# A two-layer graph kernel: every engine in source order, dense rows beside the y blocks, nonzero counts on ScalarE

## Chip, cores, metric

One core of a Trainium2 chip. The metric is the device time of one execution in microseconds (us). The engines are called PE (TensorE), ACT (ScalarE), DVE (VectorE), POOL (GpSimd) and SP (SyncE, which here only issues transfers).

## The reference

2708 nodes with 1024 features, a sparse 0/1 adjacency matrix whose row degrees vary strongly, fp32 throughout:

```python
# layer 0: attention over the neighbours
q = x @ W_q.T + b_q;  k = x @ W_k.T + b_k;  v = x @ W_v.T + b_v
z = (q @ k.T) / sqrt(1024) * adj
z = where(z == 0.0, -10000.0, z)
x = layernorm(x + relu(softmax(z, axis=1) @ v))
# layer 1: plain graph convolution
x = layernorm(x + adj @ (x @ weight) + bias)
```

## The kernel before

It never forms the 2708 x 2708 scores. It computes M = W_q^T W_k once and y = x M + ... for 22 blocks of 128 rows ("y blocks", stored to DRAM as `y_d`). From each adjacency row it lists up to 24 neighbours, and it sorts the rows by degree into 22 blocks with 23, 11, 8, 7, ... 1, 0 neighbour slots. In each layer it gathers neighbour rows by indirect transfer, weights and sums them on DVE, turns the sum by transposes on PE, multiplies by W_v (or layer 1's weight) on PE, normalizes, and scatters. The 32 rows of highest degree (`HUB`) are worked as dense matrix products instead.

The lists and the y blocks (cuts are marked):

```python
            def list_columns(b):
                r0, n = b * P, rows[b]
                a = ix.tile([P, N], F32, name="a")
                load_rows(a, adj, r0, n)
                nc.vector.tensor_scalar(junk[:n], a[:n], 0.0, None, op0=ALU.not_equal, op1=ALU.add,
                                        accum_out=cnt[:n, b:b + 1])
                nc.vector.scalar_tensor_tensor(a[:n], a[:n], 1.0, iota[:n], op0=ALU.is_equal, op1=ALU.mult)
                # [cut: maxima of six ranges, then the 24 largest]

            def y_block(b):
                # [cut: loads of xt and xn, junka sums on ACT]
                nc.vector.scalar_tensor_tensor(junkc[:n], xn[:n], 1.0, u_bc[:n], op0=ALU.mult, op1=ALU.mult,
                                               accum_out=yo[:n, D:D + 1])
                nc.gpsimd.tensor_tensor(yo[:n, D:D + 1], yo[:n, D:D + 1], beta[:n], ALU.add)
                for h in range(NH):
                    hs = slice(h * HALF, (h + 1) * HALF)
                    po = p_o.tile([P, HALF], F32, name="po")
                    for c in range(DC):
                        nc.tensor.matmul(po, xt[:, c, :], m_sb[:, c, hs], start=(c == 0), stop=(c == DC - 1))
                    nc.vector.tensor_add(yo[:n, hs], po[:n], y_bc[:n, hs])
                m = n // 16 * 16
                nc.scalar.dma_start(out=y_d[r0:r0 + m], in_=yo[:m])
                if m < n:
                    nc.scalar.dma_start(out=y_d[r0 + m:r0 + n], in_=yo[m:n])
```

The end of the sort, the loop that mixes lists, y blocks and sort, and the norm that closes every block of both layers:

```python
                for b in range(NB):
                    put = nc.gpsimd.indirect_dma_start(
                        out=tab_d[:, :], out_offset=bass.IndirectOffsetOnAxis(ap=pos_i[:, b:b + 1], axis=0),
                        in_=rec[:, b, :], in_offset=None)
                    tc.declare_no_dep(put.ins, group="tab", reason="disjoint rows: positions are unique")
                    tc.add_to_no_dep_group("tab", put.ins)
                nc.sync.dma_start(out=tabs, in_=tab_d.rearrange("(b p) e -> p b e", p=P))

                for g in range(G):
                    nc.sync.dma_start(out=hub_row[g * HUB:(g + 1) * HUB], in_=tab_d[0:HUB, ROW:ROW + 1])
                for g in range(G):
                    gs = slice(g * HUB, (g + 1) * HUB)
                    nc.vector.tensor_scalar(hub_i[gs], hub_row[gs], float(G), float(g), op0=ALU.mult, op1=ALU.add)
                # [cut]
            for b in range(NB):
                for k in (2 * b, 2 * b + 1):
                    if k < NB:
                        list_columns(k)
                y_block(b)
                if 2 * b + 2 == NB:
                    sort_rows()

        def norm(t, sm, n):

            nm = stat.tile([P, 1], F32, name="lnm")
            nc.vector.tensor_scalar_mul(nm[:n], sm[:n], -1.0 / D)
            vs = stat.tile([P, 1], F32, name="vs")
            nc.scalar.activation(junks[:n], t[:n], AF.Square, bias=nm[:n], accum_out=vs[:n])
            ve = stat.tile([P, 1], F32, name="ve")
            nc.vector.tensor_scalar(ve[:n], vs[:n], 1.0 / D, EPS, op0=ALU.mult, op1=ALU.add)
            rstd = stat.tile([P, 1], F32, name="rstd")
            nc.gpsimd.tensor_tensor(rstd[:n], ve[:n], negh[:n], ALU.pow)
            nmr = stat.tile([P, 1], F32, name="nmr")
            nc.gpsimd.tensor_tensor(nmr[:n], nm[:n], rstd[:n], ALU.mult)
            nc.scalar.activation(t[:n], t[:n], AF.Identity, bias=nmr[:n], scale=rstd[:n])
```

The dense rows' scores are part of layer 0's jobs, and layer 1's residual add is on POOL at the block's end:

```python
        jobs = [17, 0, "hub", 16, 0, 15, 0, "one", 14, 1, ...]     # [cut]

        def finish1(b, po, xr):                                     # layer 1
            # [cut]
                nc.gpsimd.tensor_tensor(xr[:n], xr[:n], bias1[:n], ALU.add)
                # [cut: two evictions on DVE, each adding xr and summing]
            norm(t, sm, n)
            scatter(out, b, n, t, "out")
```

The source above is not the order in which an engine works: without a further word, the builder's scheduler reorders the instructions of each engine. With `tc.manual_schedule()` each engine issues them as the source has them.

## Time and profile before

| what | before |
|---|---|
| time, median of 4 runs beside the changed kernel | 1364.74 us (1360.12 to 1367.37) |
| weights and M; y blocks | 155.7 us; to 495 us |
| layer 0; layer 1 | 450 us; 389 us |
| busy PE, DVE, POOL, ACT | 1195.5, 802.4, 503.5, 284.2 us |
| mean granted PE clock | 0.928 |

The lines of the page, the stage windows and PE's waits of this kernel are in the prediction below. Read them so: PE is busy 88% and is the engine to feed. A wait line names the engine, what it wanted to do, what it waited for, the total, how often, and the longest. The main reading below compares DVE's waits inside layer 0. Here are three of them in this kernel:

```profile
DVE t L521 <- PE po L419: 69.2, 12, 16.4
DVE junkv L439 <- DMA g<-in_x_dram,tabs: 30.2, 19, 8.3
...
DVE ve L431 <- ACT junks L429: 6.9, 6, 1.3
```

They are the wait for PE's product, for gathered rows, and for ACT's Square (the sum of squares in `norm`).

### The profile page before, as it was taken

The numbers are of one execution on the slowest core, as the hardware profiler recorded it, in microseconds if no ns is written. First come the engines' busy times: TensorE is split into PE (matmuls) and PEld (weight loads), VectorE is DVE, ScalarE is ACT, GpSimd is POOL, SyncE is SP. The second block draws the span as 40 slices with busy tenths as digits, with TensorE's granted clock in tenths as the row PEclk, the third lists the DMA queues.
The fourth block names the chain that finished last, engine by engine and source line by source line (L and its number), as shares of the span: only waits on it lengthen the run. The fifth ranks groups of instructions, "written<-read, shape, count | busy, mean of one in ns | idle before, by whom it ended". The sixth has DMA issues, their size and how long they took to land. (4 is left out here: it accounts for less than half of the span.)

```text
span 1361.2 us, 10176 instructions
## 1 busy us (share of the span) xinstructions
PE 1195.5 (88%) x3225; PEld 542.9 (40%) x3225; DVE 802.4 (59%) x1448; ACT 284.2 (21%) x697; POOL 503.5 (37%) x494
## 2 busy tenths in 40 slices
PE   6999978899989996987891999997788899988996
PEld 4544433344434442442250444443332344433442
DVE  5899989993131216795078898941452355656611
ACT  2300101122121212221021233232110113121321
POOL 1000000000600036362167677511773558778711
PEclk7899989899999997998986899999888899988998
DMA  7434376534254359868778787711889866677511
GB/s 288 144 134 152 141 298 233 173 121 139 63 158 119 82 208 416 343 220 241 202 282 278 256 278 249 253 46 47 277 289 298 272 221 210 232 227 237 184 47 49
DMA packets 92391, 275.79 MB, mean 203 GB/s; under 512 B 12372, under 2 KB 34228, under 8 KB 88596
## 3 DMA queue, kind: packets, MB, share of 16 engines
q0 software_dynamic: 44896, 160.96, 34.5%
q1 hardware_dynamic: 44368, 102.95, 23.8%
q10 hardware_dynamic: 3064, 11.14, 2.1%
q8 instruction: 27, 0.44, 0.1%
q14 instruction: 36, 0.29, 0.1%
HBM read 241.38 MB, written 33.63 MB: 202 GB/s over the span
## 5 line engine op out<-in xcount | busy, mean ns | idle before, releaser
L279 PE MATMUL po<-m_sb,xt 128*128 128x512 f32 x704 | 312.2, 606 | 23.0 <-DMA xt<-in_xT_dram 23.0
L419 PE MATMUL po<-wv_sb,rT 128*128 128x512 f32 x704 | 317.8, 607 | 1.7 <-DVE rT L657 1.7
L419 PE MATMUL po<-w_sb,rT 128*128 128x512 f32 x672 | 303.4, 607 | 17.1 <-DVE t L737 17.1
L279 PEld LDWEIGHTS po<-m_sb,xt 128*128 128x128 f32 x704 | 136.3, 195 | 196.2 <-issue 177.7
L419 PEld LDWEIGHTS po<-wv_sb,rT 128*128 128x128 f32 x704 | 134.0, 195 | 170.0 <-issue 164.7
L419 PEld LDWEIGHTS po<-w_sb,rT 128*128 128x128 f32 x672 | 127.8, 194 | 177.6 <-issue 162.4
L381 POOL DMA_INDIRECT g<-in_x_dram,tabs x122 | 151.0, 1238 | 96.7 <-issue 46.1
L721 DVE SCALAR_TENSOR_TENSOR r<-g,valid,r 128x1024 f32<-128x1024 f32 x79 | 126.5, 1602 | 66.9 <-DMA g<-x_d,tabs 65.2
L381 POOL DMA_INDIRECT g<-x_d,tabs x122 | 140.8, 1154 | 34.4 <-issue 29.9
L439 DVE SCALAR_TENSOR_TENSOR junkv<-yg,g 128x1024 uint8<-128x1024 f32 x100 | 122.3, 1223 | 31.0 <-DMA g<-in_x_dram,tabs 30.2
L433 POOL TENSOR_TENSOR rstd<-ve,negh 128x1 f32<-128x1 f32 (+1 forms) x44 | 39.6, 901 | 222.9 <-DVE ve L431 222.7
L429 ACT ACTIVATE junks<-t,lnm 128x1024 uint8<-128x1024 f32 (+1 forms) x44 | 50.6, 1150 | 327.8 <-DVE lnm L427 323.5
L220 PE MATMUL po<-wk_o,wq_o 128*128 128x512 f32 x256 | 112.3, 598 | 0.0
L264 ACT ACTIVATE junka<-xt 128x128 f32<-128x128 f32 x176 | 54.4, 309 | 258.2 <-DMA xt<-in_xT_dram 197.8
L487 DVE SCALAR_TENSOR_TENSOR r<-g,pr,r 128x1024 f32<-128x1024 f32 x79 | 100.5, 1282 | 6.9 <-ACT r L485 6.3
L271 POOL MEMSET yo<- 128x4 f32 x22 | 2.2, 102 | 267.4 <-DMA y_d<-yo 205.7
L410 PE MATMUL tr<-ident,r 128*128 128x128 f32 x336 | 51.2, 300 | 53.3 <-DVE e L460 28.6
L436 ACT ACTIVATE t<-t,nmr,rstd 128x1024 f32<-128x1024 f32 (+1 forms) x44 | 54.6, 1240 | 144.8 <-POOL nmr L435 140.4
L272 DVE SCALAR_TENSOR_TENSOR junkc<-xn,u_bc 128x1024 uint8<-128x1024 f32 (+1 forms) x22 | 26.9, 1224 | 92.6 <-POOL yo L271 72.0
L249 DVE MAX8 few<-a 128x8 f32<-128x75 f32 (+3 forms) x132 | 76.9, 614 | 0.1
L737 DVE SCALAR_TENSOR_TENSOR t<-po,g 128x512 f32<-128x512 f32 x42 | 28.4, 686 | 79.4 <-PE po L419 79.4
L521 DVE TENSOR_TENSOR t<-po,bias_bc 128x512 f32<-128x512 f32 (+1 forms) x44 | 30.2, 686 | 75.4 <-PE po L419 75.4
(189 smaller groups left out, 948.5 us busy)
## 6 DMA issues: line engine op xcount, KB each, us to landing
a<-in_adj_dram SPq DMA_DIRECT2D x21, 1354.0 KB
xm<-in_xT_dram SPq DMA_DIRECT2D x8, 1354.0 KB
y_d<-yo ACTq DMA_DIRECT2D x21, 514.0 KB
xt<-in_xT_dram SPq DMA_DIRECT2D x21, 512.0 KB
xn<-in_x_dram SPq DMA_DIRECT2D x21, 512.0 KB
g<-in_x_dram SPq DMA_DIRECT2D x24, 448.0 KB
g<-x_d SPq DMA_DIRECT2D x24, 448.0 KB
wq_i<-in_wqT_dram SPq DMA_DIRECT2D x8, 512.0 KB
```

The source lines that it names most:

```text
L220: nc.tensor.matmul(po, wq_o[:, o, i * P:(i + 1) * P], wk_o[:, o, hs], start=(o == 0), stop=(o == DC - 1))
L249: nc.vector.max(few[:n, i * 8:(i + 1) * 8], a[:n, cuts[i]:cuts[i + 1]])
L264: nc.scalar.activation(junka[:, :P], xt[:, c, :], AF.Copy, accum_out=xs[:, c, b:b + 1])
L279: nc.tensor.matmul(po, xt[:, c, :], m_sb[:, c, hs], start=(c == 0), stop=(c == DC - 1))
L381: nc.gpsimd.indirect_dma_start(out=g[:n], out_offset=None, in_=src, in_offset=bass.IndirectOffsetOnAxis(ap=tabs[:n, b, word:word + 1], axi ...
L410: nc.tensor.transpose(tr[:, k, :], r[:, c * P:(c + 1) * P], ident)
L419: nc.tensor.matmul(po, rT[:, c, :], w[:, c, h * HALF:(h + 1) * HALF], start=(c == 0), stop=(c == DC - 1))
L429: nc.scalar.activation(junks[:n], t[:n], AF.Square, bias=nm[:n], accum_out=vs[:n])
L436: nc.scalar.activation(t[:n], t[:n], AF.Identity, bias=nmr[:n], scale=rstd[:n])
L439: nc.vector.scalar_tensor_tensor(junkv[:n], yg[:n, :D], scale, xg[:n], op0=ALU.mult, op1=ALU.mult, accum_out=s)
L487: nc.vector.scalar_tensor_tensor(r[:n], xg[j][:n], pr[:n, j:j + 1], r[:n], op0=ALU.mult, op1=ALU.add)
L721: nc.vector.scalar_tensor_tensor(r[:n], xg[:n], valid[:n, b, j:j + 1], r[:n], op0=ALU.mult, op1=ALU.add)
```

## The change

The intent was to replace the scheduler's order by one planned by hand. PE is to find its next operand ready at every step, and the dense rows' work is to be taken out of layer 0, where they caused PE's longest waits.

```diff
-    with es:
+    with es, tc.manual_schedule():
```
```diff
+            nc.scalar.activation(junk[:n], a[:n], AF.Sign, accum_out=cnt[:n, b:b + 1])
+            nc.scalar.activation(junk[:n], a[:n], AF.Relu, scale=-1.0, accum_out=neg[:n, b:b + 1])
-                nc.vector.tensor_scalar(junk[:n], a[:n], 0.0, None, op0=ALU.not_equal, op1=ALU.add,
-                                        accum_out=cnt[:n, b:b + 1])
```

On ACT the count takes two passes: the Sign pass counts, and the Relu pass finds rows with negative entries, for which that count would not hold.

```diff
+EARLY = 13      # lists beside M; the other nine in y blocks 0 to 6
+SORT = 7        # sort around the eighth y block
+G1, G2 = 6, 8   # gather buffers (15 before); adjacency buffers 2 -> 3, xn 2 -> 1, r 4 -> 3, yg 3 -> 2
+        for b in range(SORT):
+            while done < EARLY + (NB - EARLY) * (b + 1) // SORT:
+                list_columns()
+                done += 1
+            y_block(b)
+        sort_begin()
+        y_block(SORT)
+        sort_end()
+        # [cut]
+        for b in range(SORT + 1, NB):
+            y_block(b)
+            # [cut: at chosen b, one piece of the dense rows: scores in 24 steps, softmax, two chunks of rows]
+        wv_sb = wv_pool.tile([P, DC, D], F32, name="wv_sb", tag="v")
+        nc.sync.dma_start(out=wv_sb, in_=wvT.rearrange("(c p) n -> p c n", p=P))
```

The body of both layers becomes one loop. `work.run()` issues the next job's gathers and then computes the job issued before. A job is one or several pieces of at most eight neighbours of a block.

```diff
+            for i, b in enumerate(order):
+                xr = residual(b)                       # gather, POOL
+                credit += STEP - end_cost
+                # [cut: work.run() until the next block is there, and while there is credit]
+                for h in range(NH):
+                    product(b, turned[b], h, po)       # 16 matmuls
+                    if h == 0 and i + 1 < len(order):
+                        turned[order[i + 1]] = turn(order[i + 1])   # transposes on PE, copies on ACT
+                for hook in hooks.get(i, ()):
+                    hook()                             # a chunk of the dense rows
+                if past is not None:
+                    end(*past)                         # finish0 or finish1 of the block before
+                past = b, po, xr
```

Between the scatters of the sort a one-element memset was added on POOL as a spacer.

## The prediction

> **What bounds the kernel now.** I read the busy shares and the 40 slices first, then TensorE's waits, then busy time by stage, then each engine's timeline around the waits.
>
> ```profile
> PE 1195.5 (88%) x3225; PEld 542.9 (40%) x3225; DVE 802.4 (59%) x1448; ACT 284.2 (21%) x697; POOL 503.5 (37%) x494
> PE   6999978899989996987891999997788899988996
> DVE  5899989993131216795078898941452355656611
> PEclk7899989899999997998986899999888899988998
> ```
>
> TensorE leads; the rest is its idle time (166 us) and the clock it loses after each gap. Where DVE shows 9 (slices 3 to 10 and 20 to 25), TensorE dips.
>
> The stages, as windows cut where TensorE's operand changes (columns: window, length, busy time per engine, granted clock, DMA share, GB/s):
>
> ```profile
> 0.00:155.70 155.70, 140.75 (x409) 73.22 (x410) 135.78 (x258) 28.58 (x70) 3.55 (x11) 0.91 0.48 175
> 155.70:320.00 164.30, 145.24 (x331) 63.93 (x330) 142.12 (x272) 30.92 (x148) 5.77 (x20) 0.94 0.57 194
> 320.00:495.00 175.00, 169.70 (x398) 75.08 (x396) 39.17 (x94) 36.58 (x178) 26.16 (x46) 0.99 0.38 110
> 495.00:945.00 450.00, 382.61 (x1137) 172.38 (x1138) 300.48 (x569) 109.42 (x189) 226.50 (x206) 0.92 0.72 245
> 961.00:1350.00 389.00, 356.24 (x951) 157.55 (x949) 181.09 (x247) 73.76 (x107) 233.33 (x202) 0.94 0.66 216
> ```
>
> They are: weights and M; y blocks 0 to 9; y blocks 10 to 21; layer 0; layer 1. At full clock the timeline of TensorE has 0.43 us per fp32 matmul instruction, so 13.7 us a y block (32 of them) and 14.6 a block of the layers (with transposes). Layer 0 needs 22 x 14.6 = 321 us plus some 45 for the dense ("hub") rows, and takes 450. Layer 1 needs 21 x 14.6 = 307 plus 31, and takes 389. So 80 and 50 us are there to be won. The y blocks lose 36, and I expect the turn between the layers (16) and the tail (11) to stay. TensorE's waits, whole run:
>
> ```profile
> PE tr L410 <- DVE e L460: 28.6, 1, 28.6
> PE po L279 <- DMA xt<-in_xT_dram: 23.0, 4, 8.2
> PE po L419 <- DVE t L737: 17.1, 5, 5.8
> PE tr L410 <- DVE r L719: 16.2, 2, 15.1
> PE tr L403 <- DVE part L610: 14.5, 2, 8.7
> PE mm L553 <- DMA yg<-y_d,tabs: 10.2, 1, 10.2
> PE po L607 <- DMA g<-in_x_dram: 7.8, 1, 7.8
> ```
>
> The dense rows in layer 0 bring the waits on yg, g and part, and behind them DVE falls late (28.6).
>
> **What the Trainium skill says.** (1) TensorE: Matmul & The Clock Gate, Part 1: after an idle window of about 3.4 us the array runs at half rate until about 3.4 us of work. The trace agrees: the eight transposes after the 15 us gap at 960 took 1.94 us, later ones 1.04. A long gap therefore costs about 2 us more than itself. (2) The same page, "Architectural detail": ACT and DVE are strict FIFO, and TensorE only pulls weight loads ahead. The trace of before agrees as far as it goes: ACT's junka waited 21.3 us on DVE's yo, because the y_d transfer stood ahead of it in ACT's order. This decides my prediction: source order makes every wait hold all that stands behind it. (3) DMA: Bandwidth & Descriptors, "Anatomy of one DMA": a semaphore wait happens on the issuing sequencer. SP's waits agree (151 us behind DVE's few). (4) ScalarE: Activation LUTs, "Step-by-step": 0.833 ns per element for any function. Here 128x128 took 309 ns and 128x1024 took 1150, a slope of 0.94; I use that.
>
> **Part by part.**
>
> *Weights and M.* All 32 groups of transposes now precede M. A pair took 2.65 us: 7.3 + 16 x 2.65 = 50; M is 256 x 0.43 = 110, plus 2 of cold clock: 162, against 155.7. The count leaves DVE (21 x 2.95 = 62 us), and ACT gets two passes of 2708: 1.15 + 1684 x 0.94 ns = 2.73, plus 0.19 for the sum, so 5.9 us a list. Thirteen lists fit beside M (8.4 us apart; DVE needs 2.97 + 3.3 for the maxima + 1.0). The last list's passes stand ahead of the y_bc copies on ACT, so y block 0 starts near 170.
>
> *y blocks 0 to 7, nine lists among them.* Here I see a closed ring. ACT reaches the passes of the next list only after the y_d issue of this block, which waits for DVE's eviction; DVE may overwrite `a` only after ACT's passes; SP, in order, loads the next adjacency block only when the maxima are done, and xn (now one buffer) behind it; DVE needs xn before it evicts. The landing time is in the timeline:
>
> ```profile
> 220.44 0.33 SPq L144 DMA_DIRECT2D a<-in_adj_dram  x1
> 220.87 0.38 SPq L260 DMA_DIRECT2D xt<-in_xT_dram  x1
> 227.91 0.31 ACT L264 ACTIVATE junka<-xt 128x128 f32<-128x128 f32 x1 [15.88 <-DMA xt<-in_xT_dram]
> ```
>
> Half a megabyte behind an adjacency block landed 7.5 us after the first issue; I take 7.2. Round the ring: 0.5 (issue) + 5.9 + 6.25 + 7.2 + 1.25 (junkc) + 1.35 (eviction) = 22.5 us, 7.3 more with two lists, 16.3 when no adjacency load is left (23.6 with two). Evictions end at 193, 215, 238, 268, 290, 306, 330. TensorE, two blocks ahead at most, wants 13.7 and starves.
>
> *Sort.* Before, the positions to the tables was:
>
> ```profile
> 342.76 1.15 POOL L339 DMA_INDIRECT tab_d<-rec,pos_i  x1 [0.17 <-issue]
> 369.65 0.97 POOL L339 DMA_INDIRECT tab_d<-rec,pos_i  x1 [0.30 <-issue]
> 371.80 0.38 SPq L344 DMA_DIRECT2D tabs<-tab_d  x1
> 375.96 0.14 DVE L350 TENSOR_SCALAR hub_i<-hub_row 32x1 int32<-32x1 int32 x1 [3.35 <-DMA hub_row<-tab_d]
> ```
>
> That is 33 us, and the scheduler had put evictions between. In source order hub_i follows at once on DVE, so no eviction passes, and xn of block 8 waits on SP behind the tables and five xm loads. Sort start and block 7 end at 339; 6.6 of DVE, 29 to 30 of POOL, 6 of landing, 9 until xn lands, 3 of junkc and eviction: block 8 is evicted near 394. TensorE has two blocks (27 us) to fill 55. Blocks 0 to 9, done at 320 before, are done at 394.
>
> *Blocks 10 to 21 with the dense rows.* 12 x 13.7 = 165, 2 cold, and TensorE's dense work: two dozen score steps 10, hub_y 128 small matmuls at 0.11 = 14, transposes and flips 5, two chunks of rows 8, waits for softmax and copies 8: 45. Ends at 606. Then wv (4 MB) is issued only after the last block and behind row chunks: 6.3 MB at some 380 GB/s (the slices peak at 416) is 17 us, about 18 idle: 624.
>
> *Layer 0.* The dense stalls are gone, but DVE still has 100 scores x 1.30 + 79 sums x 1.28 + 66 for the 22 ends + some 30 small = 327 us, against TensorE's 321 + 20 for the remaining chunks. In order, each end's variance waits for ACT's Square, about 1.5 us (22.4 us over 17 waits before), so DVE needs 327 + 33 + 15 for gathers = 375, little of it done in the wv gap. Layer 0: 376 instead of 450, ends near 1000. *Turn* 15. *Layer 1*: 338 plus 12 of waits, since POOL needs (J+1) x 1.43 + 6.9 us a block, over 14.6 for J above 4: 350 instead of 389. *Tail* 12.
>
> Sum: 606 + 18 + 376 + 15 + 350 + 12 = 1377. Gains 74 + 39; losses 6 + 74 + 38 + 18. I have counted each wait as fully exposed; xn's rows are contiguous and may land 2 to 3 us sooner, six times, and layer 0 may run nearer TensorE's 341. I take 22 off: **1355 us**.
>
> **Rivals.** (A) The plan holds: TensorE never waits over a few us; y and dense rows end near 520, layer 0 takes 345, layer 1 345: about 1250. For it: idle and cold clock are all that separates the stages from their work, and the parameters look tuned. Against: the ring and the hub_i wait follow from order alone. (B) In-order DVE is worse than I think in layer 0: each residual gather, exp and Square stops it; DVE's 300 us busy took 390 before with free order. Layer 0 then stays near 430: about 1420. (C) The wait for tables is mostly covered and the ring is as computed: 1310.
>
> **Range and chances.** A and C below, B above, my sum at 1377 as it stands: 1280 to 1415. Faster by over 2% means below 1339: 0.40; between 1339 and 1394: 0.38; slower: 0.22.
>
> **What would show it.** Right: evictions of y blocks 1 to 4 some 22 us apart; DVE waiting on ACT's passes (near 6 us) and on xn; one DVE wait of over 30 us on hub_row, a TensorE gap of 25 to 30 behind it; a gap of 15 to 20 on wv; no wait on yg or part; layer 0 under 400. Wrong: y blocks 13.7 us apart from the start (rival A), or layer 0 over 420 with DVE waiting on junks (rival B).

## The result, and the profile after

1557.37 us, median of 4 runs (1555.97 to 1558.47), against 1364.74. The ratio is 1.1415, with a 95% interval of 1.1378 to 1.1452: slower.

The page of the kernel after, its busy line, two of its 40-slice rows and the granted clock:

```profile
PE 1210.8 (78%) x3415; PEld 564.3 (36%) x3415; DVE 744.7 (48%) x1416; ACT 397.6 (26%) x785; POOL 497.4 (32%) x521
...
PE   7998976574999983967742487899485878899896
...
DVE  5899554822102211377557477776114425443321
...
PEclk9999997887989996978876789999797888999998
```

PE's work has hardly grown (15 us), but its share of the span fell from 88% to 78%: the change added idle time. The mean granted clock fell from 0.928 to 0.881.

The stage windows of the kernel after, cut where PE's operand changes (M; y blocks 0 to about 9; the rest with the dense rows; layer 0; layer 1; columns as in the prediction):

```profile
0.00:139.70 139.70, 131.86 (x402) 66.12 (x403) 111.44 (x214) 81.48 (x84) 3.48 (x10) 1.00 0.53 197
139.70:370.00 230.30, 155.02 (x342) 68.18 (x340) 118.60 (x281) 81.76 (x189) 27.89 (x64) 0.84 0.38 125
370.00:592.00 222.00, 212.42 (x767) 107.37 (x767) 41.01 (x79) 46.27 (x226) 3.88 (x26) 0.93 0.51 144
618.80:1099.40 480.60, 354.48 (x952) 164.95 (x952) 310.27 (x550) 104.49 (x170) 215.82 (x203) 0.86 0.56 194
1120.40:1545.00 424.60, 356.71 (x954) 157.65 (x954) 154.71 (x278) 75.16 (x107) 229.55 (x198) 0.91 0.57 194
```

PE's longest waits, whole run of the kernel after:

```profile
PE tr L465 <- DVE r L542: 93.0, 8, 38.7
PE po L324 <- DVE yo L325: 54.2, 5, 27.7
PE po L797 <- DVE t L891: 39.3, 10, 8.3
PE po L797 <- DVE t L578: 33.1, 3, 14.9
...
PE po L797 <- DMA wv_sb<-in_wvT_dram: 26.5, 1, 26.5
```

The waits on yg and part in layer 0 are gone, as planned. In their place PE waits for DVE: for the row sum it is to transpose (r, 93.0 us) and for PSUM, where its products gather, to be evicted, that is copied out by DVE (54.2, 39.3 and 33.1 us). Here is every wait of DVE inside layer 0 of the kernel after:

```profile
DVE junkv L494 <- DMA g<-in_x_dram,tabs: 69.4, 16, 32.3
DVE ve L486 <- ACT junks L484: 46.1, 21, 7.5
DVE r L542 <- ACT r L540: 22.8, 18, 1.6
DVE t L578 <- PE po L797: 17.6, 4, 6.2
DVE rden L532 <- ACT pr L527: 7.6, 16, 0.8
DVE den L529 <- ACT pr L527: 1.9, 3, 0.6
```

They add up to 165.4 us. With the 310.3 us that DVE is busy in this window that is 475.7 of its 480.6 us. (Work and waits fill the window of any engine, so this sum alone does not make DVE the bound.) What points to DVE is who waits for whom: in this window DVE waits for PE 17.6 us, and PE waits for DVE 126.1 (93.0 and 33.1). In the kernel before, DVE waited 69.2 us for PE's product in layer 0.

One of the waits for Square, seen in the timeline of layer 0 of the kernel after (start, duration, engine, line, instruction, and in brackets the idle time before it and what ended it):

```profile
856.11 0.15 DVE L482 TENSOR_SCALAR lnm<-sm 128x1 f32<-128x1 f32 x1
...
861.35 1.07 ACT L466 COPY rT<-tr 128x512 f32<-128x512 f32 x2 [10.60 <-PE tr L465]
...
862.31 1.16 ACT L484 ACTIVATE junks<-t,lnm 128x1024 uint8<-128x1024 f32 x1
...
863.59 0.15 DVE L486 TENSOR_SCALAR ve<-vs 128x1 f32<-128x1 f32 x1 [7.33 <-ACT junks L484]
...
863.83 1.50 POOL L488 TENSOR_TENSOR rstd<-ve,negh 128x1 f32<-128x1 f32 x1 [10.46 <-DVE ve L486]
```

DVE has the mean at 856.1. ACT could take the square of 1.15 us at once, but ahead of it in ACT's order stand the two copies of the next block's transposes, which wait for PE. The square starts at 862.3; DVE, whose next instruction needs its sum, stands 7.33 us, and POOL, which needs DVE's result, stands 10.46 us with the next gathers behind it. The later waits for gathers (69.4 us in all) may be partly made here; e4 below, which takes most of the waits for Square away, lowers them by only 9.7 us.

And DVE's longest wait in the whole kernel after, and one block end of layer 1 with an instance of it:

```profile
DVE t L891 <- POOL g L887: 175.5, 20, 31.1
...
1304.80 0.94 POOL L433 DMA_INDIRECT g<-x_d,tabs  x1 [0.30 <-issue]
1305.76 2.34 POOL L887 TENSOR_TENSOR g<-g,bias 128x1024 f32<-128x1024 f32 x1
1308.14 0.69 DVE L891 SCALAR_TENSOR_TENSOR t<-po,g 128x512 f32<-128x512 f32 x1 [11.91 <-POOL g L887]
```

POOL's add of residual and bias needs nothing that is late. But it is in the source after the next jobs' gathers, so POOL issues those first, about 1.25 us apart. PE's finished product waits in PSUM, and DVE waits 11.91 us for an add of 2.34 us. Over layer 1 this wait comes 20 times and takes 175.5 us of DVE's time.

### The profile page after: what moved, and what is told of

Read it like the earlier page. It is cut to its first block, busy times and chain, and to the rows that moved or that the text cites. A ratio compares the mean times of both kernels' runs of the same rounds, so it can differ in the third digit from the quotient of the medians. Undisturbed runs are those within 1.5% of the kernel's fastest.

```text
span 1556.6 us, 10644 instructions
## 1 busy us (share of the span) xinstructions
PE 1210.8 (78%) x3415; PEld 564.3 (36%) x3415; DVE 744.7 (48%) x1416; ACT 397.6 (26%) x785; POOL 497.4 (32%) x521
## 5 line engine op out<-in xcount | busy, mean ns | idle before, releaser
L797 PE MATMUL po<-wv_sb,rT 128*128 128x512 f32 x704 | 323.5, 618 | 59.6 <-DVE t L578 33.1
L324 PE MATMUL po<-m_sb,xt 128*128 128x512 f32 x704 | 322.6, 619 | 54.2 <-DVE yo L325 54.2
L797 PE MATMUL po<-w_sb,rT 128*128 128x512 f32 x672 | 312.2, 621 | 39.4 <-DVE t L891 39.3
L433 POOL DMA_INDIRECT g<-in_x_dram,tabs x125 | 130.2, 1042 | 106.8 <-PE mm L697 42.3
L494 DVE SCALAR_TENSOR_TENSOR junkv<-yg,g 128x1024 uint8<-128x1024 f32 x100 | 122.5, 1225 | 71.8 <-DMA g<-in_x_dram,tabs 69.4
L433 POOL DMA_INDIRECT g<-x_d,tabs x122 | 118.0, 967 | 75.3 <-issue 35.1
L488 POOL TENSOR_TENSOR rstd<-ve,negh 128x1 f32<-128x1 f32 (+1 forms) x44 | 49.2, 1118 | 240.5 <-DVE ve L486 240.4
L891 DVE SCALAR_TENSOR_TENSOR t<-po,g 128x512 f32<-128x512 f32 x42 | 27.4, 689 | 177.1 <-POOL g L887 175.5
L873 DVE SCALAR_TENSOR_TENSOR r<-g,valid,r 128x1024 f32<-128x1024 f32 x79 | 101.5, 1284 | 8.8 <-DMA g<-x_d,tabs 6.3
L466 ACT COPY rT<-tr 128x512 f32<-128x512 f32 (+1 forms) x84 | 45.5, 581 | 219.6 <-PE tr L465 219.4
L317 DVE SCALAR_TENSOR_TENSOR junkc<-xn,u_bc 128x1024 uint8<-128x1024 f32 (+1 forms) x22 | 26.9, 1223 | 140.9 <-DMA xn<-in_x_dram 137.3
L465 PEld LDWEIGHTS tr<-ident,r 128*128 128x128 f32 x336 | 43.7, 155 | 138.3 <-issue 136.1
L217 DVE SCALAR_TENSOR_TENSOR a<-a,iota 128x2708 f32<-128x2708 f32 (+1 forms) x22 | 65.3, 2968 | 42.3 <-ACT junk L216 42.3
```

Source lines behind the costliest of these rows:

```text
L433: nc.gpsimd.indirect_dma_start(out=dst[:n], out_offset=None, in_=src, in_offset=bass.IndirectOffsetOnAxis(ap=at, axis=0))
L465: nc.tensor.transpose(tr[:, k, :], r[:, c * P:(c + 1) * P], ident)
L494: nc.vector.scalar_tensor_tensor(junkv[:n], yg[:n, :D], scale, xg[:n], op0=ALU.mult, op1=ALU.mult, accum_out=s)
L797: nc.tensor.matmul(acc, rT[:, c, :], w[:, c, h * HALF:(h + 1) * HALF], start=(c == 0), stop=(c == DC - 1))
L873: nc.vector.scalar_tensor_tensor(r[:n], xg[j - cut[i]][:n], valid[:n, b, j:j + 1], r[:n], op0=ALU.mult, op1=ALU.add)
```

## The experiments

My theory after the result was ORDER: the loss is source order itself, in which each wait holds all that stands behind it on its engine, and most of it lies in the two layers (Square, and POOL's add). Its rivals were that the plan's contents cost the time whatever the order (the dense rows beside the y blocks, fewer buffers, counts on ACT), and that single stage gaps (tables, wv) or the ring in the first y blocks carry it.

**e1, the order alone.** The changed kernel with the scheduler's order:

```diff
-    with es, tc.manual_schedule():
+    with es:
```

> The changed kernel with its plan, buffers and operations as they are, but the instruction order of each engine left to the scheduler again (one word taken out). Theory ORDER (the loss comes from strict source order: waits that hold what stands behind them): DVE's waits on POOL's residual add (175 us), on the tables (33) and on Square (80) mostly go, both layers come under 450 and 390, and the time is 1290 to 1400. Rival PLACE (the loss comes from where the plan puts work and from its smaller gather buffers): stays above 1480, with the same waits under other names.

Measured 1349.94 us, ratio to before 0.9905 (0.9874 to 0.9935): 207 us less than with source order. Layer 0 took 422 us (528 to 950), layer 1 took 362 (973 to 1335). Two of DVE's waits in layer 0 of this run:

```profile
DVE junkv L494 <- DMA g<-in_x_dram,tabs: 37.7, 21, 5.0
...
DVE ve L486 <- ACT junks L484: 8.2, 7, 1.3
```

The wait for Square in layer 0 is 8.2 us instead of 46.1, by order alone; over the whole run it is 36.6 instead of 79.9, and DVE's wait for POOL's add is 26.1 instead of 175.5. This shows that source order costs the whole loss, and that the plan under a free order is about 1% from the kernel before.

**e2, source order on the kernel before**, with the same spacers as the change:

```diff
-    with es:
+    with es, tc.manual_schedule():
```

> The kernel before, all else unchanged, in strict source order (and one small memset before each table scatter, which the order needs to build). ORDER: it is slowed by 10% or more, since its source was written for a scheduler: 1500 to 1750. PLACE: within 4% of the kernel before, 1310 to 1420.

Measured 2073.14 us, ratio 1.5214 (1.5166 to 1.5262). The direction was expected, the size was above my range: PE waited 445.9 us for DVE's row sums alone, and layer 0 took some 860 us. So the plan is a good deal better than a source never meant to be issued as it stands (2073 to 1557). It just does not reach what the scheduler does with either source.

**e3, POOL's add earlier.** The add of residual and bias moved ahead of the next block's residual gather and jobs:

```diff
+                if ready is not None and past is not None:
+                    ready(*past)                # the POOL add of the block before
                 xr = residual(b)
```

> The changed kernel with POOL's add of residual and bias in layer 1 issued one step earlier, ahead of the next gathers in POOL's order; nothing else. If DVE's 175 us of waiting for that add is what makes layer 1 long (425 us), layer 1 falls to 360 to 390 and the time by 35 to 65 us, to 1490 to 1525. Rival: POOL is simply full in layer 1 (230 us busy and waits of its own round its ring), the wait moves to gathers, and the time falls by less than 15 us.

Measured 1506.19 us, ratio 1.1041: 51 us less than after. Layer 1, from the start of its first product to that of its last, took 370 instead of 422 us, and DVE's wait for this add fell from 175.5 to 30.1 us. A third of the wait taken away became time. DVE had slack in layer 1 (154.7 us busy of 424.6), and part of it came back as waits for gathers (the first row's from 38.0 to 70.7 us).

**e4, the norm in two parts.** The variance, its power, the scaling and the scatter are issued after the next step's jobs, so that DVE has other work while ACT squares. It needs a fourth `r` buffer (the kernel before had four too), so a fixed order has to be planned together with its buffers; the fourth buffer without the move was not run.

```diff
             nc.scalar.activation(junks[:n], t[:n], AF.Square, bias=nm[:n], accum_out=vs[:n])
+            return t, nm, vs, n
+        def norm_end(t, nm, vs, n):
             ve = stat.tile([P, 1], F32, name="ve")
 ...
+                flush()                         # norm_end and scatter of the block before
                 po = []
```

> The changed kernel with each block's normalisation cut in two: the part behind ACT's Square (variance, rstd, scaling, scatter) is issued one step later, after the next step's gathers and sums; one more r buffer, which that needs. If the chain DVE-ACT-DVE-POOL in the middle of the queues costs what the waits say (DVE 80 us on Square, POOL 225 on the variance, which holds the gathers), DVE's wait on Square falls under 15, its wait on gathers in layer 0 (69) at least halves, and the time falls by 50 to 110 us. Rival: those waits only fill slack that the busiest engine leaves: less than 20 us.

Measured 1471.97 us, ratio 1.0791: 85 us less, the largest single term. From first to last product layer 0 took 430 instead of 480 us, and layer 1 386 instead of 422. In the whole run:

```profile
DVE junkv L497 <- DMA g<-in_x_dram,tabs: 59.7, 14, 30.7
...
DVE ve L489 <- ACT junks L484: 25.7, 11, 6.8
```

The wait for Square fell from 79.9 to 25.7 us, not under 15 as expected (in layer 0 alone it is 6.1). The waits for gathers fell from 69.4 only to 59.7, so the part of my expectation that had them halve missed too.

**e5, wv earlier.** W_v and the bias loaded before y block 18 instead of after the last.

```diff
         for b in range(SORT + 1, NB):
+            if b == SORT + 11:
+                # bias_bc and wv_sb: tile and load, moved here from after the loop
             y_block(b)
```

> The changed kernel with the loads of wv and its bias issued four y blocks earlier on SP; nothing else. ORDER: the 26.5 us that TensorE waits for wv, and the cold clock behind it, go: 22 to 30 us less, 1527 to 1536. Rival: layer 0 is bound by DVE, which has the gap to catch up, so that a later wait gives it back: less than 10 us.

Measured 1555.38 us, ratio 1.1427 (1.1396 to 1.1458): 2 us less than after by the medians, but in e5 to e8 the kernel before was also 3.5 us faster (1361.26), and the kernel after was not run again. By the ratio (1.1415 for the kernel after) nothing is gained, which is what the rival expected (under 10 us). PE's wait of 26.5 us on wv is gone, and in its place in the waits of PE stands this one:

```profile
PE po L798 <- DVE rT L807: 17.1, 1, 17.1
```

DVE reaches rT only after the single-neighbour blocks, whose gathers come late: POOL stood 13.37 us until PE had used a chunk of the dense rows and its gather buffers came free. Two waits lay side by side; taking one away left the other. The last product of the y blocks also began 9 us later.

**e6, tables later.** The load of the sorted tables and hub_i moved behind y block 10, so that DVE could evict while POOL scatters.

```diff
+            if b == SORT + 3:
+                sort_tabs()                     # tabs, hub_row, hub_i, degs, valid
+                # the gathers of a0 and x0 and the first load_xm, moved here
```

> The changed kernel with the part of the sort behind the table scatters (reading the tables, hub_i, valid, the two dense gathers, the first xm loads) issued three y blocks later. ORDER: DVE's 33 us wait on hub_row and TensorE's 27.7 us gap behind it go, 24 to 34 us less, 1523 to 1534. Rival: the dense rows then start later and push into layer 0: under 10 us.

Measured 1552.29 us, ratio 1.1401 (1.1376 to 1.1425): 5 us less by the medians, 2 by the ratio, and so not clear of noise. PE's gap of 27.7 us went down to 8.7. But DVE did not evict while POOL scattered. In place of its 33.3 us for hub_row stands:

```profile
DVE junkc L317 <- POOL yo L316: 28.3, 1, 28.3
```

This is the next block's memset of `yo`, which stands in POOL's order behind the scatters. So the wait changed its name and lost only 5 us; what it would be worth if it were gone was not tested. New waits of PE of 6.0 and 5.2 us came for the rows gathered later, so layer 0 began at 611.5 instead of 618.8 us, and two more us were given back behind it.

**e7, the ring opened.** ACT stores a y block only after the next list's passes, and xn of the next block is loaded before the next adjacency block.

```diff
+            while stores:
+                stores.pop(0)()                 # y_d issue, after the next Sign and Relu
 ...
             load_x()
+            if b < SORT:
+                load_xn(b + 1)
```

> The changed kernel with the ring of the first y blocks opened at two places: each xn load is issued ahead of the next adjacency load on SP, and the y_d store of a block behind the next list's two passes on ACT; nothing else. ORDER: of the 42 us that TensorE waits in y blocks 3 to 7 (and at the sort) 30 or more go, 30 to 50 us less with the cold clock: 1507 to 1527; DVE's 137 us wait on xn falls by 70 or more. Rival: DVE's lists themselves are the bound there: under 15 us.

Measured 1501.8 us, ratio 1.1036: 55 us less by the medians, 52 by the ratio, a little more than expected. Layer 0 began at 563.2 instead of 618.8 us, so all that was won in the y blocks was kept. DVE's wait for ACT's passes fell from 42.3 to 8.5 us; its wait for xn fell from 137.3 only to 115.1, where I had expected 70 less. (A wait of 28.4 us on an eviction, that of the tables, is still there.) This shows the ring of the prediction and its price.

**e8, all five together**, still in source order: the edits of e3 to e7.

> The changed kernel, still in source order, with all five moves at once: residual add early, normalisation in two parts, wv early, tables late, ring open. ORDER: the single gains (51 and 85 measured, some 25, 28 and 40 expected) add up, less some 20 that two of them share: 1330 to 1370, level with the kernel before. Rival: each freed wait only uncovers the next: above 1420.

Measured 1389.76 us, ratio 1.0212 (1.0192 to 1.0233): 168 us less than after, where the single gains add up to 198. It stayed 20 us above the range that I had given. Layer 1 took 365 us (362 in free order). Layer 0 took 429 from its first to its last product (480 in the kernel after, 430 in e4, 422 in e1). Two of DVE's waits in this layer 0, and the window, which runs 7 us past the start of the last product:

```profile
DVE junkv L517 <- DMA g<-in_x_dram,tabs: 54.6, 11, 26.5
...
DVE ve L509 <- ACT junks L504: 7.5, 5, 1.6
```

```profile
556.00:992.00 436.00, 346.93 (x952) 160.24 (x952) 310.90 (x555) 103.38 (x173) 190.61 (x207) 0.90 0.62 218
```

The wait for Square is down to 7.5 us. DVE's 310.9 us and all its waits (111.0) make 421.9 of these 436 us, of which its waits for gathers are the half. One wait of PE is new here: it waits for ACT's copies of the transposes, 26.0 us in layer 0, where the kernel after has none:

```profile
625.45 1.24 ACT L514 ACTIVATE t<-t,nmr,rstd 20x1024 f32<-20x1024 f32 x1 [2.33 <-POOL nmr L513]
626.59 1.04 ACT L486 COPY rT<-tr 128x512 f32<-128x512 f32 x2
627.21 8.56 PE L837 MATMUL po<-wv_sb,rT 128*128 128x512 f32 x16 [18.28 <-ACT rT L486]
```

The second part of the norm, which e4 moved, now puts ACT's scaling of one block, which needs DVE's variance and POOL's power, ahead of the copies for the next. So the move took away one wait of this kind and made another; a better place for it was not tried.

**e9, all five in the scheduler's order** (e8 without `tc.manual_schedule()`).

> The changed plan with all five moves in the source, and the order left to the scheduler. If the moves help it as they help source order, 1300 to 1335, below both kernels. Rival: the scheduler already placed these instructions so, and layer 0 is held by DVE (297 us busy in 431): within 1% of the free order without them, 1337 to 1363.

Measured 1348.35 us, ratio 0.9917 (0.9881 to 0.9952), the same as e1. With its own order the scheduler gains nothing from the five edits, as the rival expected.

**e10, e11, e12, the counts alone.** e10 is e1 with the counts put back on DVE; e11 is the kernel before with only the counts moved to ACT; e12 is the changed kernel with the counts put back on DVE. The edit of e11:

```diff
-                nc.vector.tensor_scalar(junk[:n], a[:n], 0.0, None, op0=ALU.not_equal, op1=ALU.add,
-                                        accum_out=cnt[:n, b:b + 1])
+                nc.scalar.activation(junk[:n], a[:n], AF.Sign, accum_out=cnt[:n, b:b + 1])
+                nc.scalar.activation(junk[:n], a[:n], AF.Relu, scale=-1.0, accum_out=neg[:n, b:b + 1])
 ...
+                nc.vector.scalar_tensor_tensor(capn, neg, 0.0, capn, op0=ALU.is_gt, op1=ALU.max)
```

> Free order, with the nonzero counts put back on DVE (62 us more there, 119 us less on ACT). If the counts are worth something, DVE's lists end later, the sort with them, and the time rises by 10 to 30 us over the free order, 1360 to 1380. Rival: DVE has slack in the y blocks (128 us busy of 371), under 7 us.

> The kernel before with only the nonzero counts moved to ACT. There DVE was full from 68 to 300 us and SP's loads of xt waited behind its lists (TensorE waits 23 us on xt): 8 to 25 us less than before, 1338 to 1356. Rival: the y blocks lose only what xt's landing costs anyway, under 5 us.

> The changed kernel in source order with the counts back on DVE. In the ring of the first y blocks 5.9 us of ACT become 2.95 of DVE, some 27 us less over nine lists; beside M the list takes DVE 10.3 us against 8.4 between two, so DVE comes some 25 us late out of M: within 20 us of the changed kernel, 1537 to 1577. Rival (the passes on ACT are what makes the ring long): 30 us or more less.

Measured: e10 1370.44 us, ratio 1.0077 (1.0045 to 1.011); e11 1337.66 us, ratio 0.9838 (0.9803 to 0.9872); e12 1575.96 us, ratio 1.1587 (1.1546 to 1.1629). Moving the counts to ACT is worth about 20 us in every order, by the medians: 22 in the kernel before, 20 in free order (e10 against e1, of another call), 19 in source order (e12 against the kernel after, of another call); by the ratios, 22 to 23 in each. In e11 the gain of 1.6% is clear of noise. In e11 the y blocks end at 468 us instead of 493. PE's wait there for its operand was 23.0 us in the kernel before; with the counts on ACT it is:

```profile
PE po L281 <- DMA xt<-in_xT_dram: 4.3, 1, 4.3
```

The likely chain, not tested further: DVE finishes each list sooner, the two adjacency buffers come free sooner, and SP, which loads both in turn, reaches the next xt sooner. The counts are the only part of the change that was shown to gain. The rest of the plan together costs about 10 us in free order: e1, which has the counts on ACT too, takes 1350, and e9 1348, where e11 takes 1338.

**e13, e14, e15, what still holds layer 0.** Open after e8 was whether layer 0 is held by (a) the order of the heavy blocks, whose work comes before DVE has any lead, or (b) the number of gather buffers. e13 is e8 with the heavy blocks two places later. e14 is e11 with the same order. In both, the list of jobs is moved with it (not shown). e15 is e8 with `G2` 10 instead of 8.

```diff
-        order = last + single[::-1] + [17, 16, 15, 0, 14, 1, 13, 2, 12, 3, 11, 4, 10, 5, 9, 6, 8, 7]
+        order = last + single[::-1] + [17, 16, 15, 14, 13, 0, 12, 1, 11, 2, 10, 3, 9, 4, 8, 5, 7, 6]
```

> All five moves in source order, and in layer 0 the 23-slot block two places later, the other heavy blocks one light block later each. (a) early DVE work holds layer 0: the one wait of 36 us behind that block shrinks to under 15 and the time falls by 15 to 35 us, 1355 to 1375. (b) gather buffers: within 8 us of 1390.

> The kernel before with the counts on ACT and the same later place of the heavy blocks in layer 0. (a): the 28.6 us wait behind that block mostly goes: 12 to 30 us less than the counts alone, 1308 to 1326, below every version so far. (b): within 6 us of 1338.

> All five moves in source order with 16 gather buffers instead of 14. (b): DVE's wait on gathers in layer 0 falls by 20 us or more and the time by 10 to 25, 1365 to 1380. (a): within 6 us of 1390.

Measured: e13 1388.72 us, ratio 1.0189 (1.0165 to 1.0213); e15 1386.45 us, ratio 1.0181 (1.0153 to 1.0208); both the same as e8. In e13 PE's single wait of 36.0 us on DVE became several of at most 8.5 us, and one of 11.9 on ACT came up: PE's waits in layer 0 are 91.4 us in all against 100.2, and the time is the same. In e15 DVE waited 55.7 us for gathers against 54.6. So neither (a) nor (b) holds; what does was not tested. PE's waits for ACT's copies are in both runs (27.1 and 24.9 us). e14 took 1332.18 us, ratio 0.9785 (0.9762 to 0.9809). It has the lowest median of all, ahead of both kernels of the case, but is only about 5 us below e11, where I had expected more, and the two ran in different calls. Whether the later heavy blocks gain anything over e11 stays open.

## Why the prediction was wrong

Predicted 1355 us with 1280 to 1415; measured 1557. The sum before my discount was 1377. By its own terms:

| step | predicted | measured | difference |
|---|---|---|---|
| weights and M | 162 | 139.7 | -22 |
| y blocks 0 to about 9 | 232 (to 394) | 230.3 (to 370) | -2 |
| the other y blocks, dense rows | 212 | 222 | +10 |
| wait for wv | 18 | 26.5 | +8 |
| layer 0 | 376 | 480.6 | +105 |
| turn | 15 | 21 | +6 |
| layer 1 | 350 | 424.6 | +75 |
| tail | 12 | 11.6 | 0 |

The differences and the 22 us taken off make 202, all of the miss.

- *Right: the ring.* Evictions of the first y blocks began at 171.3, 192.9, 214.5, 243.6, 263.9, 279.5 and 302.6, so they are 21.6, 21.6, 29.1, 20.3, 15.6 and 23.1 us apart; I had 22, 23, 30, 22, 16 and 24, some 20 us later, as M ended sooner than I had it. DVE's waits for ACT's passes were 5.3 us on average over eight, and for xn near 6 in the first blocks (137.3 over all 17). e7 shows that opening the ring gives 55 us.
- *Right: the wait for the tables, and its gap.* DVE waited 33.3 us on hub_row in one piece, and PE 27.7 us behind it. What it was worth is not shown, since in e6 DVE waited 28.3 us for POOL in its place. The wv gap was 26.5 instead of 18, and taking it away (e5) won nothing clear of noise, because another wait lay beside it; my sum had booked it in full.
- *Wrong, in the good direction: M.* I carried the 2.65 us per pair of transposes over. In the kernel after a pair took 1.44 us, and M started at 29.6 instead of 50. The traces differ in PE's granted clock there: before, it was 0.50 from 18 to 39 us, after a wait of 4.10 us, and the eight transposes of a pair took 1.97 us; after, it was 1.00 and they took 1.09. Why the kernel after has no such wait was not tested.
- *Off in two readings and a sum, without weight.* TensorE does not dip in most slices where DVE shows 9 (in slices 3 to 5 both show 9). The losses "6 + 74" count M's 6 us twice, as 394 minus 320 has them in it; the stage sum 1377 does not. And the slope of 0.94 ns for ACT mixes two forms: the Trainium skill, "ScalarE: Activation LUTs", What ACT_TABLE_LOAD costs, gives 186 + 0.833 N ns for immediate operands and about 280 + 0.833 N with a bias pointer. Estimated from these figures, the Sign pass with N = 2708 takes 2442 ns; it took 2462, where I had 2730. Square with N = 1024 takes 1133 by the same estimate; it took 1150.
- *The step that failed: "DVE needs 327 + 33 + 15 for gathers = 375".* The mechanism was named, DVE in order with waits inside. The work was even over-estimated (310 instead of 327). The waits were 165 instead of 48: gathers 69.4 instead of 15 (the kernel before already had 30.2 us on scores and 14.1 on the single-neighbour blocks); Square 46.1 instead of 33; and exponentials, the first scaled row on ACT and PE's products 49.9, which I had not counted. I took the length of Square's wait from the kernel before, where under the scheduler's order it was some 1.3 to 1.5 us each time. In source order it stands behind copies that wait for PE, 7.33 us in the instance shown. In e4, where the wait for Square in layer 0 is 6.1 us, layer 0 is 50 us shorter.
- *Also failed: "338 plus 12 of waits" for layer 1.* I had added up POOL's work per block (its issue rate) but not asked in which order POOL does it: the add behind the next gathers. DVE waited 175.5 us for this add where I had 12 us of waits in all, and e3 takes 51 us of the 75 back by moving that one line.
- *Rival B* named the right engine and the right stage ("layer 0 over 420 with DVE waiting on junks"), and e1 and e4 support it; its 1420 was too small, as it had layer 0 at 430 and left layer 1 out. Rival A's clean plan is not reached even by e8.
- *The discount.* I took 22 us off for waits that might be hidden. The one on wv was (e5), but in the same model the layers' waits were counted too few.

What stays open: where e8 loses its last 40 us to e1. Only 7 of them are in layer 0 (429 against 422 us) and 3 in layer 1. 28 lie before layer 0, which begins at 556.0 us in e8 and at 528.4 in e1; 17.5 of these are PE's wait for rT, the one that e5 uncovered. No experiment took that wait away. In layer 0 the order of blocks and two more buffers do not change the time; a shorter DVE list, or another place for the second part of the norm, was not tried.

## What to carry to other kernels

Before fixing the order of every engine by hand, walk each engine's list and ask of each instruction what it waits for and what stands behind it. A 1 us square behind two copies that wait for PE, or a 2 us add behind nine gathers, made waits of many times its own length (7.33 and 11.91 us), and the scheduler here avoided most of them without being asked (e1). When DVE or ACT is near the bound, sum its work and its in-order waits per stage, not its work alone; here the work was 17 us less than predicted, and the waits were 165 us instead of 48. After moving an instruction, look whether its wait is gone or only stands under another name, as in e6. And try the cheap part of a large change by itself: moving the count from DVE to ACT gained 1.6% alone, and was hidden under a loss of 14% in the whole.

## What the Trainium skill lacked or had wrong

- "TensorE: Matmul & The Clock Gate", Architectural detail, says that ACT and DVE are strict FIFO. It does not say what that can cost: the same source took 1557 us in source order and 1350 with the scheduler's order (e1), and the kernel before 2073 against 1365 (e2).
- I know of no page that tells how far the worth of a wait can lie from its length: a PE wait of 26.5 us went and the time stayed the same within noise (e5), while 85 us came with waits for Square that fell by only 54.2 (e4).
